# When the expert weights are laid out, and where layer 1's gate is folded, in a two-layer attention and mixture-of-experts kernel

## The chip, the core and the metric

The kernel runs on one core of one Trainium2 chip, as one launch. The metric is device time in microseconds (us), the median of the runs shown. Engines are named as in the profile: PE (TensorE, matrix products), PEld (its weight loads), DVE (VectorE), ACT (ScalarE), POOL (GpSimd), SP (SyncE, which here only starts transfers). ACT and POOL start transfers too (ACTq, POOLq). SBUF is the on-chip memory with 128 partitions; PSUM holds the results of PE in eight banks.

## What is computed

The input `x` holds 8 sequences of 256 tokens with 512 features, in float32. Two layers are added to it, one after the other.

```python
x = x + ffn0(attention(x, Wq, Wk, Wv, Wo, norms, cached keys and values, table, kv_lens))
x = x + moe1(lora(x, W, A, B, scalings, adapter_idx))

# ffn0: each token takes its best 2 of 8 experts, weights rw by softmax
weighted = (softmax(expert_atom_weights) @ atoms) * sigmoid(importance)   # (8, 4096)
vals = einsum('tk,tks->ts', rw, weighted[top_idx])
out = xt @ W.T + segment_sum((xt[:, mask_idx % H] * vals).T, mask_idx // H).T

# moe1: gate by softmax, best 2 of 8 experts
h = gelu(einsum('th,ehi->eti', x, fc1_w) + fc1_b)
y = einsum('eti,eih->eth', h, fc2_w) + fc2_b
out = einsum('eth,te->th', y, combine)
```

So layer 0's expert `e` is a dense 512 x 512 matrix (`W.T` plus 4096 scattered entries of its own), and layer 1's input passes a projection with a low-rank adapter chosen per sequence.

## The kernel before

**Start.** Token tiles hold 128 tokens, so there are 16. `keys_values(i)` (line 908) projects tile `i` to keys and values, four products of 512 columns. `base_weights(i)` spreads the shared matrix `W` over the eight experts into `delta_d`, an array in device memory with experts innermost; `add_delta` (line 882) adds the scattered entries into it by indirect transfers, which run on until batch 5 of attention. Ahead of the first `keys_values`, line 959 transposes the softmaxed `expert_atom_weights` (`pe`) and line 961 copies it to `eawT`, which is first needed by the products at line 978.

**Attention.** A loop over the 8 batches (line 1277) calls `attend(b, 0, ...)` and `attend(b, 1, ...)` (line 1154), each for 128 queries. An `attend` goes through four pairs of heads `m`: scores on PE (line 1162), mask and maximum on DVE (1177), exponential with sum on ACT (1193), division on DVE (1204), transposes on PE (1207) with their copy `pT` on ACT (1211), products with the values on PE (1216) and a copy of the result `oT` on either ACT or DVE (`nc.any`, 1226). Beside it run the queries of batch `b + 2` (up to batch 5), the gate products (`gate_rows`), and the output rows of the first `EARLY = 9` tiles (`output_rows`, line 385: four products into `ph`, an ACT copy to `h`, a transfer to `h_d` from ACT's queue). `start_sums(b - 1)` (line 1268) reads `x` rows and writes them to `sums_d[0]`, where layer 0's output is accumulated.

**Layout of the expert weights.** Layer 0's products need the weights with experts outermost. `load_delta(half, pool, engines)` (line 372) does that for half of the weights in 8 steps: SP reads 512 KB of `delta_d` into a buffer `raw` (line 380), and an engine copies it, transposed within each partition, into `delta[half]` (line 381). The first half is called in batch 6 (line 1285), with ACT's copy alone and three buffers shared with the query inputs; the second half (line 1452) behind the gate's fold, with POOL and ACT in turn and two buffers.

**Between attention and layer 0's slots.** Routing constants; the output rows of tiles 9 and 10; `top2`, `shifted_exp` and `route` (line 136), a long DVE chain that ends in a matrix `put`; inside it the output rows of tiles 11 to 15; then products `pm` (line 250) that give the row numbers `token_i` and the weights of each slot. `fold_gate` (line 1325) follows: layer 1's gate is applied ahead of layer 1's projection, so its weights are folded into it. It loads the projection's weights `wc` (1 MB), transposes them (`pw` to `wn`, lines 1345 and 1346), multiplies them with the gate (`pgw`, 1402), adds the adapters' part (`pga`, 1411) and writes `aTg`; it also prepares the adapters (`aT`, `bT`, `an`, `bn`, `pick`, and `GB` from `pgb`, 1379; `pbg`, 1391).

**Layer 0's slots.** A slot holds 128 routed rows of one expert (line 1489): POOL gathers the rows from `h_d` by `token_i` (`fetched`, line 328), PE transposes them (`pa`, `turned`, 341), eight matmul instructions multiply with `delta` (1501), ACT scales (1511), POOL adds the result into `sums_d` (`added`, 348). Meanwhile SP loads layer 1's weights (`w1`, `w2_0`) and ACT's queue `wc` again. The 36 slots end in a run-time branch (line 1517) for further slots.

**Layer 1.** `sums_d` is read back (line 1544) and added on DVE (1545), transposed (`turn`, 1551), multiplied with `aTg` for the gate's inputs (`inner`, `px`, 1558), then projected (`outer`, 1593). After a second `route`, 36 slots of two products each (lines 1667 and 1695) end the kernel.

**What sets the order.** Each engine has one queue in order. The order is written when the program is built: a planner goes by the place in the program and by when it reckons that inputs are there, and lets later work that it holds for ready pass earlier work. `tc.keep_in_program_order(ins)` ties an instruction behind the one written just before it on the same engine, in issue order only. Memory is reused by tile: a tile waits for the users of the tiles that lay at its addresses.

Of the kernel before, what the change touches and what calls it, by code (L numbers as in the profile page):

```python
# [11 lines left out]
F32 = mybir.dt.float32  # L12
# [41 lines left out]
def two_layer_kernel(ctx: ExitStack, tc: tile.TileContext, io: dict, out: bass.AP):  # L54
# [317 lines left out]
    def load_delta(half, pool, engines, tag="raw", bufs=2):  # L372

        dsrc = delta_d[: D * D, :].rearrange("(c p r) e -> c p r e", p=P, r=D)
        QD = D // 4
        for k in range(HK):
            for j in range(4):
                cols = slice(j * QD, (j + 1) * QD)
                raw = pool.tile([P, QD, E], F32, name="raw", tag=tag, bufs=bufs)
                nc.sync.dma_start(raw, dsrc[half * HK + k][:, cols, :])  # L380
                engines[j % len(engines)](
                    delta[half][:, k, :, cols], raw.rearrange("p r e -> p e r")
                )
# [17 lines left out]
    with ExitStack() as att:  # L401
# [500 lines left out]
        with proj:  # L902
# [55 lines left out]
            pe = psd.tile([P, E], F32, name="pe", tag="psd")  # L958
            nc.tensor.transpose(pe, eaw.rearrange("e h a -> e (h a)"), ident[:E, :E])
            eawT = dp.tile([P, E], F32, name="eawT")  # L960
            nc.scalar.copy(eawT, pe)
            LEAD = 3
            for i in range(LEAD):
                keys_values(i)
                base_weights(i)
            zero_e = dp.tile([P, E], F32, name="zero_e")
# [187 lines left out]
        def attend(b, t, kvs, QT, KT, mask):  # L1154
            oT = oTs[b]
            for m in range(KC):
# [69 lines left out]
                nc.any.tensor_copy(oT[:, m, t * P : (t + 1) * P], po)  # L1226

# [48 lines left out]

        for b in range(B):
# [6 lines left out]
            if b == B - 2:  # L1284
                load_delta(0, xq, (nc.scalar.copy,), tag="xb", bufs=3)
# [3 lines left out]
            if b > 0:  # L1289
                start_sums(b - 1)  # L1290
            if b == B - 1:
                start_sums(b)
            if b == 1:
                for rest in (*sums_d, h_d, g_d):
                    nc.sync.dma_start(rest[N:, :], zero)
            attend(b, 0, kvs, QTs[b], *ready)
# [14 lines left out]
            attend(b, 1, kvs, QTs[b], *now)  # L1311
# [8 lines left out]
    def load_cond(pool):  # L1320
        wc = pool.tile([P, KC, D], F32, name="wc")
        nc.scalar.dma_start(wc, io["w1T"].rearrange("(c p) o -> p c o", p=P))
        return wc

    def fold_gate(fold, ps_t, ps_x):
        wc = load_cond(fold)
# [3 lines left out]
        nc.scalar.dma_start(bT, io["bT"])  # L1330

        wn = fold.tile([P, KC, D], F32, name="wn")
        an = fold.tile([P, D], F32, name="an")
        bn = fold.tile([P, KC, P], F32, name="bn")
        for dst, src in (
            (an, [aT[:, k, :] for k in range(KC)]),
            (bn.rearrange("p c r -> p (c r)"), [bT[:, k * P : (k + 1) * P] for k in range(KC)]),
            *(
                (wn[:, o, :], [wc[:, k, o * P : (o + 1) * P] for k in range(KC)])
                for o in range(KC)  # L1340
            ),
        ):
            pw = ps_t.tile([P, KC, P], F32, name="pw", tag="misc")
            for k in range(KC):
                nc.tensor.transpose(pw[:, k, :], src[k], ident)
            nc.any.tensor_copy(dst, pw.rearrange("p c r -> p (c r)"))
        gw1 = fold.tile([P, KC, E], F32, name="gw1")
        nc.scalar.dma_start(gw1, io["gate1"].rearrange("(c p) e -> p c e", p=P))
# [23 lines left out]
        pick = fold.tile([P, B, BW], F32, name="pick")  # L1372
# [4 lines left out]
        for g in range(B // 4):  # L1377
            pgb = ps_t.tile([P, D], F32, name="pgb", tag="misc")
# [9 lines left out]

        pbg = ps_x.tile([P, E], F32, name="pbg", tag="misc")
# [8 lines left out]
        gwc = fold.tile([P, KC, E], F32, name="gwc")  # L1398
        for d in range(KC):
            pgw = ps_x.tile([P, E], F32, name="pgw", tag="misc")  # L1400
            for k in range(KC):
                nc.tensor.matmul(
                    pgw,
                    wn[:, k, d * P : (d + 1) * P],
                    gw1[:, k, :],
                    start=(k == 0),
                    stop=(k == KC - 1),
                )
            nc.vector.tensor_copy(gwc[:, d, :], pgw)
            pga = ps_x.tile([P, B, BW], F32, name="pga", tag="misc")  # L1410
# [16 lines left out]
    with ExitStack() as ffn:  # L1427
        tp = ffn.enter_context(tc.tile_pool(name="tp0", bufs=1))
        lp = ffn.enter_context(tc.tile_pool(name="lp", bufs=2))
        ps_r = ffn.enter_context(tc.tile_pool(name="ps_r", bufs=1, space=PSUM))  # L1430
        ps_t = ffn.enter_context(tc.tile_pool(name="ps_t", bufs=2, space=PSUM))
        ps_f = ffn.enter_context(tc.tile_pool(name="ps_f", bufs=2, space=PSUM))
# [17 lines left out]
        fold_gate(fp, ps_t, ps_f)  # L1450

        load_delta(1, lp, (nc.gpsimd.tensor_copy, nc.scalar.copy))
# [66 lines left out]
    dst_.close()  # L1519
# [3 lines left out]
    rp = ctx.enter_context(tc.tile_pool(name="rp", bufs=1))  # L1523
# [4 lines left out]
    with ExitStack() as cond:  # L1528
        xtp = cond.enter_context(tc.tile_pool(name="xtp", bufs=1, side="right"))
        x1T = xtp.tile([P, KC, N], F32, name="x1T")  # L1530
        xab = cond.enter_context(tc.tile_pool(name="xab", bufs=4, side="right"))
        ps_t = cond.enter_context(tc.tile_pool(name="ps_t1", bufs=1, space=PSUM))
        ps_l = cond.enter_context(tc.tile_pool(name="ps_l", bufs=1, space=PSUM))
        ps_c = cond.enter_context(tc.tile_pool(name="ps_c", bufs=5, space=PSUM))
# [43 lines left out]
        def outer(q, xa):  # L1578
# [12 lines left out]
            for i, pc in zip(quads[q], pcs):  # L1591
# [8 lines left out]
                g = xab.tile([P, D], F32, name="g", bufs=2)  # L1600
# [213 lines left out]
```

## Time and profile before

| what | value |
|---|---|
| median of 3 runs | 1011.23 us (1009.95 to 1013.35) |
| the profiled execution | 1016.23 us, span of its core 1014.4 us, mean granted PE clock 0.953 |
| busy in the span | PE 942.2, PEld 514.2, DVE 441.1, ACT 382.7, POOL 366.2 us |
| start, keys and values | 0 to 92 us |
| attention, batches 0 to 7 | to 409.7 us |
| up to layer 0's first slot matmul | to 467.98 us |
| layer 0's slots | to 605.9 us |
| up to `outer`'s last product | to 708.5 us |
| layer 1's slots, end | from 724.25 us |
| all transfers | 137.13 MB, mean 135 GB/s |

In a row of the stage table stand the stage (us from the span's start), its length, then for each engine its busy time and, behind an x, its instructions, then the clock granted to PE (1.00 is full), the mean busy share of the 16 DMA engines and what they moved. In a list of waits stand the waiting instruction, its releaser, the total of the waits, how many, and the longest. In a timeline row stand the start, the time from first start to last end, the engine, the line, the operation with its names (out<-in), shapes and count; the bracket gives the idle time of the engine before it and what ended it. Matmuls of float32 appear as several instructions each.

### The profile page before, as it was taken

What the parts mean: (1) busy time and instruction counts of PE and PEld (TensorE: products, weight loads), DVE (VectorE), ACT (ScalarE), POOL (GpSimd) and SP (SyncE); (2) the same over time, 40 slices, a digit from 0 to 9 for tenths busy, and PEclk for the clock granted to TensorE, in tenths of its full rate; (3) what the DMA queues carried; (4) which work ended last, traced back from release to release, by engine and by line L of the source; (5) the groups of instructions that cost most, each with busy time, mean ns of one, the idle gap of its engine ahead of it and who ended that gap; (6) DMA issues with size and microseconds to landing.
All of it is one profiled execution on the core that took longest, in us unless ns stands there. A gap on an engine that the chain in (4) does not pass through costs nothing. (4 is left out here: it accounts for less than half of the span.)

```text
span 1014.4 us, 13280 instructions
## 1 busy us (share of the span) xinstructions
PE 942.2 (93%) x4145; PEld 514.2 (51%) x4145; DVE 441.1 (43%) x1437; ACT 382.7 (38%) x946; POOL 366.2 (36%) x320
## 2 busy tenths in 40 slices
PE   5999889999998899979999985999599999999996
PEld 2655646556555466455444443453245445444542
DVE  5689689855846676832111113440022222222221
ACT  3577356646648878322111111311122222222221
POOL 2622656565463100233667640000233333333321
PEclk9799689999999999998999995999699999999998
DMA  6597492332224600656998759842432333333222
GB/s 186 171 322 276 118 331 60 97 95 74 63 53 120 223 2 1 200 165 206 343 287 158 137 84 296 314 158 73 156 62 55 73 63 61 63 72 63 54 33 38
DMA packets 75654, 137.13 MB, mean 135 GB/s; under 512 B 17710, under 2 KB 23342, under 8 KB 75457
## 3 DMA queue, kind: packets, MB, share of 16 engines
q0 software_dynamic: 25984, 45.26, 23.3%
q1 hardware_dynamic: 38496, 74.57, 21.4%
q10 hardware_dynamic: 11104, 16.44, 4.5%
q8 instruction: 36, 0.59, 0.2%
q14 instruction: 34, 0.27, 0.1%
HBM read 92.05 MB, written 53.61 MB: 144 GB/s over the span
## 5 line engine op out<-in xcount | busy, mean ns | idle before, releaser
L1667 PE MATMUL ph<-w,xsT 128*128 x288 | 131.6, 600 | 0.2 <-issue 0.2
L328 POOL DMA_INDIRECT xs<-g_d,token_i_l x36 | 37.4, 1039 | 258.1 <-PE pa L341 147.0
L1695 PE MATMUL py<-w,hs 128*128 x288 | 129.6, 592 | 0.5 <-ACT hs L1684 0.5
L1501 PE MATMUL py<-delta,xsT 128*128 x288 | 129.1, 593 | 0.3 <-ACT aTg L1414 0.3
L1703 DVE TENSOR_TENSOR y<-py,b 128x512 f32<-128x512 f32 x36 | 24.9, 692 | 211.9 <-PE py L1695 211.9
L343 DVE COPY xsT<-pa 128x512 f32<-128x512 f32 x72 | 49.5, 688 | 150.0 <-PE pa L341 138.7
L1193 ACT ACTIVATE s<-s,mx,roots 128x384 f32<-128x384 f32 x128 | 89.7, 704 | 8.6 <-DVE mx L1189 7.0
L1695 PEld LDWEIGHTS py<-w,hs 128*128 128x128 f32 x288 | 54.6, 190 | 69.2 <-issue 68.2
L1684 ACT ACTIVATE hs<-pu,b 128x128 f32<-128x128 f32 x144 | 41.0, 368 | 116.0 <-PE pu L1681 116.0
L1667 PEld LDWEIGHTS ph<-w,xsT 128*128 128x128 f32 x288 | 52.5, 193 | 52.9 <-issue 52.9
L1501 PEld LDWEIGHTS py<-delta,xsT 128*128 128x128 f32 x288 | 52.1, 190 | 53.6 <-issue 53.1
L913 PE MATMUL pkv<-wkv,xb 128*128 128x512 f32 x128 | 67.1, 650 | 8.8 <-DMA wkv<-wqkvT 8.4
L348 POOL DMA_INDIRECT out<-y,token_i_l x36 | 56.6, 1571 | 48.5 <-DVE y L1706 35.6
L1177 DVE CUSTOM_DVE_ANT_0 s<-ps,mask 128x384 f32<-128x384 f32 x128 | 67.1, 552 | 14.4 <-PE ps L1162 11.9
L348 POOL DMA_INDIRECT sums_d<-y,token_i_l x36 | 56.5, 1570 | 36.9 <-ACT y L1511 22.4
L1216 PE MATMUL po<-pT,kv 128*64 128x128 f32 x768 | 66.1, 285 | 3.4 <-ACT pT L1211 2.3
L1511 ACT ACTIVATE y<-py,weight_l 128x512 f32<-128x512 f32 x36 | 24.7, 687 | 114.1 <-PE py L1501 111.4
L1216 PEld LDWEIGHTS po<-pT,kv 128*64 128x64 f32 x768 | 46.4, 137 | 40.8 <-ACT pT L1211 32.1
L389 PE MATMUL ph<-woT,oT 128*128 128x512 f32 x128 | 60.1, 613 | 5.6 <-ACT h L397 5.6
L1675 ACT COPY h<-ph 128x512 f32<-128x512 f32 x36 | 21.1, 585 | 113.3 <-PE ph L1667 113.3
L1162 PE MATMUL ps<-KT,QT 64*128 64x384 f32 x256 | 58.8, 540 | 4.1 <-DVE mx L1177 4.0
L1211 ACT COPY pT<-pp 128x384 f32<-128x384 f32 x128 | 55.9, 477 | 17.3 <-PE pp L1207 15.5
(353 smaller groups left out, 1497.8 us busy)
## 6 DMA issues: line engine op xcount, KB each, us to landing
delta_d<-spread SPq DMA_DIRECT2D x16, 512.0 KB
raw<-delta_d SPq DMA_DIRECT2D x16, 512.0 KB
w<-fc_w SPq DMA_DIRECT2D x8, 1024.0 KB
w<-fc_w SPq DMA_DIRECT2D x16, 512.0 KB
part<-sums_d SPq DMA_DIRECT2D x32, 256.0 KB
xb<-xT SPq DMA_DIRECT2D x5, 1024.0 KB
sums_d<-zero SPq DMA_DIRECT2D x18, 256.0 KB
kv_new<-kvt ACTq DMA_DIRECT2D x16, 256.0 KB
```

Source lines behind the costliest of these rows:

```text
L343: nc.vector.tensor_copy(xsT, pa)
L348: nc.gpsimd.indirect_dma_start(out=sum_d, out_offset=bass.IndirectOffsetOnAxis(ap=token_i[:, s : s + 1], axis=0), in_=y, in_offset=None, b ...
L389: nc.tensor.matmul(ph, oTs[i // 2][:, k, (i % 2) * P : (i % 2 + 1) * P], woT[:, k, :], start=(k == 0), stop=(k == KC - 1),)
L913: nc.tensor.matmul(pkv, xb[:, k, cols], wkv[:, k, :], start=(k == 0), stop=(k == KC - 1),)
L1162: lambda r=r: nc.tensor.matmul(pss[r], QT[r * HD : (r + 1) * HD, m, t * P : (t + 1) * P], KT[r * HD : (r + 1) * HD, u, t * P : t * P + WU] ...
L1177: nc.vector.tensor_tensor_reduce(out=s, in0=pss[r], in1=mask[:, t, :], scale=1.0, scalar=NEG, op0=ALU.add, op1=ALU.max, accum_out=mx[:, r ...
L1193: nc.scalar.activation(ss[r], ss[r], AF.Exp, bias=mx[:, r : r + 1], scale=root[:, r : r + 1], accum_out=sm[:, r : r + 1],)
L1211: nc.scalar.copy(pT, pp)
L1216: lambda c=c, r=r: nc.tensor.matmul(po[r * HD : (r + 1) * HD, :], kvs[t + c][:, v0 + r * HD : v0 + (r + 1) * HD], pTs[r][:, c * P : (c + 1 ...
L1501: nc.tensor.matmul(py, xsT[:, k, :], delta[k // HK][:, k % HK, bass.ds(own[s], 1), :].rearrange("p a d -> p (a d)"), start=(k == 0), stop= ...
L1667: nc.tensor.matmul(ph, xsT[:, k, :], w1[:, k, bass.ds(own_pe[s], 1), :].rearrange("p a d -> p (a d)"), start=(k == 0), stop=(k == KC - 1),)
L1695: nc.tensor.matmul(py, hs[:, k, :], w2[k // HK][:, k % HK, bass.ds(own_pe[s], 1), :].rearrange("p a d -> p (a d)"), start=(k == 0), stop=( ...
```

## The change

1. `load_delta` becomes a generator. It first starts as many reads as it has buffers, then stops before every copy (`yield`) and starts the next read behind it. With `paced`, the copy is kept in program order.
2. The first half is started in batch 6 and advanced from `attend`, once behind every second pair of heads, in batches 6 and 7 (8 times, for 8 copies). `start_sums` runs one batch earlier, and in batch 5 for batches 5, 6 and 7 at once.
3. The second half gets 8 buffers instead of 2. All its reads are started ahead of the routing constants; its copies stay the last work of the stage.
4. `output_rows` of this stage gets 4 PSUM banks (`ps_f`) instead of 2.
5. `fold_gate` is split. `fold_adapters` stays where it was and does the adapters' part (`an`, `bn`, `pick`, `GB`, `pbg`). The rest (transposes of `wc`, `pgw`, `pga`, `aTg`) runs behind layer 0's slots and takes the `wc` that is loaded during the slots for the projection; the first load of `wc` is gone. It uses eight PSUM banks and two `wn` buffers; the memory of layer 0's weights is given back only behind it.
6. At the start, `pe` and `eawT` come behind the first `keys_values` and `base_weights`.

```diff
-    def load_delta(half, pool, engines, tag="raw", bufs=2):
+    def load_delta(half, pool, engines, bufs, tag="raw", paced=False):
-        for k in range(HK):
-            for j in range(4):
-                cols = slice(j * QD, (j + 1) * QD)
-                raw = pool.tile([P, QD, E], F32, name="raw", tag=tag, bufs=bufs)
-                nc.sync.dma_start(raw, dsrc[half * HK + k][:, cols, :])
-                engines[j % len(engines)](
-                    delta[half][:, k, :, cols], raw.rearrange("p r e -> p e r")
-                )
+        places = [(k, slice(j * QD, (j + 1) * QD)) for k in range(HK) for j in range(4)]
+        raws = []
+        def read():
+            k, cols = places[len(raws)]
+            raw = pool.tile([P, QD, E], F32, name="raw", tag=tag, bufs=bufs)
+            nc.sync.dma_start(raw, dsrc[half * HK + k][:, cols, :])
+            raws.append(raw)
+        for _ in range(bufs):
+            read()
+        for n, (k, cols) in enumerate(places):
+            yield
+            copy = engines[n % len(engines)](
+                delta[half][:, k, :, cols], raws[n].rearrange("p r e -> p e r")
+            )
+            if paced:
+                tc.keep_in_program_order(copy)
+            if len(raws) < len(places):
+                read()
...
-            pe = psd.tile([P, E], F32, name="pe", tag="psd")
-            nc.tensor.transpose(pe, eaw.rearrange("e h a -> e (h a)"), ident[:E, :E])
-            eawT = dp.tile([P, E], F32, name="eawT")
-            nc.scalar.copy(eawT, pe)
             for i in range(LEAD):
                 keys_values(i)
                 base_weights(i)
+                if i == 0:
+                    pe = psd.tile([P, E], F32, name="pe", tag="psd")
+                    nc.tensor.transpose(pe, eaw.rearrange("e h a -> e (h a)"), ident[:E, :E])
+                    eawT = dp.tile([P, E], F32, name="eawT")
+                    nc.scalar.copy(eawT, pe)
...
                 nc.any.tensor_copy(oT[:, m, t * P : (t + 1) * P], po)
+                if m % 2:
+                    next(beside, None)
...
             if b == B - 2:
-                load_delta(0, xq, (nc.scalar.copy,), tag="xb", bufs=3)
+                beside = load_delta(0, xq, (nc.scalar.copy,), 3, tag="xb", paced=True)
+                next(beside)
...
-            if b > 0:
-                start_sums(b - 1)
-            if b == B - 1:
+            if b < B - 2:
                 start_sums(b)
+            if b == B - 3:
+                start_sums(b + 1)
+                start_sums(b + 2)
...
+    def fold_gate(an, gw1, pick, wc, wns, gwc, psum, banks):
+        pgw = [psum.tile([P, E], F32, name="pgw", tag="acc", bufs=KC) for d in range(KC)]
+        for o in range(KC):
+            wn = wns.tile([P, D], F32, name="wn", tag="g", bufs=2)
+            other_side([wc[:, k, o * P : (o + 1) * P] for k in range(KC)], wn, *banks[o])
+            for d in range(KC):
+                nc.tensor.matmul(
+                    pgw[d],
+                    wn[:, d * P : (d + 1) * P],
+                    gw1[:, o, :],
+                    start=(o == 0),
+                    stop=(o == KC - 1),
+                )
         for d in range(KC):
...
-            nc.vector.tensor_copy(gwc[:, d, :], pgw)
-            pga = ps_x.tile([P, B, BW], F32, name="pga", tag="misc")
+            nc.vector.tensor_copy(gwc[:, d, :], pgw[d])
+            bank, tag = banks[d]
+            pga = bank.tile([P, B, BW], F32, name="pga", tag=tag)
...
-        lp = ffn.enter_context(tc.tile_pool(name="lp", bufs=2))
+        lp = ffn.enter_context(tc.tile_pool(name="lp", bufs=1))
-        ps_f = ffn.enter_context(tc.tile_pool(name="ps_f", bufs=2, space=PSUM))
+        ps_f = ffn.enter_context(tc.tile_pool(name="ps_f", bufs=4, space=PSUM))
+        relayout = load_delta(1, lp, (nc.gpsimd.tensor_copy, nc.scalar.copy), 8)
+        next(relayout)
...
-        fold_gate(fp, ps_t, ps_f)
-
-        load_delta(1, lp, (nc.gpsimd.tensor_copy, nc.scalar.copy))
+        folding = fold_adapters(rp0, fp, ps_t)
+
+        for _ in relayout:
+            pass
...
-    dst_.close()
...
+        with tc.tile_pool(name="ps_g", bufs=1, space=PSUM) as ps_g:
+            gwc = xab.tile([P, KC, E], F32, name="gwc", bufs=1)
+            banks = [(ps_t, "pt"), (ps_g, "misc"), (ps_l, "route_a"), (ps_l, "route_b")]
+            fold_gate(*folding, wc, xab, gwc, ps_g, banks)
+        dst_.close()
```

`other_side` holds the four transposes and the copy (`nc.any`) that `fold_gate` had in line.

## Prediction

> **What bounds the kernel now.** I read the stage table first, then the idle time, then each engine's queue in the stages that the diff touches. TensorE (PE) is busy for 942 of 1014 us, so only PE's holes and slow-clock stretches can be won. Columns: stage, its length, busy us of each engine, granted clock, DMA share, GB/s.
>
> ```profile
> core 0: us, PE busy (x) PEld busy (x) DVE busy (x) ACT busy (x) POOL busy (x), PEclk, DMA share, GB/s
> 323.60:337.60 14.00, 11.22 (x34) 5.31 (x33) 6.13 (x18) 12.27 (x16) 3.04 (x4) 0.88 0.65 209
> 337.60:350.00 12.40, 10.18 (x82) 6.40 (x83) 6.54 (x20) 11.27 (x19) 3.25 (x2) 1.00 0.68 213
> 350.00:365.00 15.00, 13.78 (x116) 9.23 (x113) 12.86 (x52) 11.50 (x31) 0.00 (x0) 1.00 0.27 101
> 365.00:388.80 23.80, 23.80 (x206) 16.40 (x205) 16.19 (x66) 19.04 (x53) 0.00 (x0) 1.00 0.00 1
> 388.80:409.70 20.90, 20.01 (x178) 13.49 (x177) 11.99 (x49) 16.11 (x46) 0.52 (x3) 1.00 0.01 2
> ...
> 430.00:440.00 10.00, 5.95 (x11) 2.61 (x12) 2.29 (x2) 2.74 (x3) 4.30 (x2) 0.89 0.64 177
> 450.00:460.00 10.00, 7.87 (x42) 5.89 (x42) 2.91 (x12) 2.34 (x4) 4.10 (x4) 0.74 0.44 125
> ...
> 608.00:612.00 4.00, 0.00 (x0) 0.00 (x0) 0.00 (x0) 0.00 (x0) 0.47 (x1) 0.56 0.65 102
> 616.00:620.00 4.00, 2.23 (x8) 1.43 (x8) 1.72 (x3) 1.17 (x2) 0.00 (x0) 0.50 1.02 313
> ```
>
> The first five rows are batches 5 (three rows), 6 and 7 of attention: PE is idle for 6.2 us in batch 5 and for 0.9 us in the other two. Then come the stage before layer 0's slots and the gap behind them, with PE idle and its clock at half. Who waits for whom from 300 to 470 us:
>
> ```profile
> ACT delta L381 <- DMA raw<-delta_d: 21.4, 8, 5.0
> DVE hot L243 <- PE pm L250: 13.1, 6, 11.7
> PEld ph L389 <- ACT h L397: 8.1, 3, 4.6
> POOL xs L328 <- DVE wn L1346: 6.8, 1, 6.8
> ```
>
> They form one chain: two raw buffers hold the reads back, so ACT stands at a layout copy that waits for its read; the copies of `h` stand behind it; PE waits for them in `ph`; routing's `pm` is queued on PE behind `ph`; the row numbers come out of `pm`. The timelines of PE and DVE show the rest:
>
> ```profile
> 14.38 0.24 PE L959 MATMUL pe<-ident,eaw 8*128 8x8 f32 x1 [2.22 <-DVE place L1006]
> 442.98 1.91 PE L250 MATMUL pm<-put,hot 128*128 128x78 f32 x16
> 455.66 0.44 PE L341 MATMUL pa<-ident,xs 128*128 128x128 f32 x1 [1.89 <-issue]
> 467.98 2.38 PE L1501 MATMUL py<-delta,xsT 128*128 x5 [0.26 <-ACT aTg L1414]
> 616.39 1.11 PE L1551 MATMUL pt<-ident,part 128*128 128x128 f32 x4 [10.52 <-DVE part L1545]
> ```
>
> ```profile
> 418.19 2.01 DVE L300 TENSOR_TENSOR coef<-coef,sm_l 128x128 f32<-128x128 f32 x1
> 424.40 2.02 DVE L189 TENSOR_SCALAR rows_i<-rows_i 128x32 int32<-128x32 int32 x1
> ```
>
> The first rows have arrived at 455.66, yet the first slot matmul starts at 467.98, behind the last `aTg` of the gate's fold.
>
> **1. The softmax transpose at the start.** `pe` stands on PE between the fourth and fifth matmul of the first token tile and idles PE for 2.2 us. Behind `keys_values(0)` its input is long there. The clock also recovers sooner: after the hole PE ran at half clock from 14.55 to 18.04. Gain at least 2.2, at most 2.2 + 1.7 = 3.9; I take 3. PE has no other hole before 92 us, so it passes on.
>
> **2. First half of the weights, paced by heads.** The eight ACT copies (2.05 us each, 16.4) now fall in batch 5, beside query matmuls, and cost its 6.2 us of PE idle and some slow clock: gain 6.5. They move to batches 6 and 7, one behind every second head, the eighth behind the last head of all. There PE is full and ACT has 19.04 + 16.11 = 35.15 of 44.7 us. Seven copies make 49.5; the 13 ACT copies of `oT` there (0.25 each), which may go to either engine, make it 46.2 if DVE takes them. So ACT becomes the bound: +1.5 to +4.8 if it never idles, +14.4 if every copy shows in full. I take +5, near the low end, because batch 5's copies cost PE only 0.8 us each, and the pin of a copy reaches back to one earlier ACT instruction, so a ready exponential may pass it. Net -1.5, between -5 and +8. The `x` rows' start moves one batch earlier, with three batches at once in batch 5: on SP it stands ahead of the raw reads, but those reads are first needed a batch later. The later raw reads each wait on SP for a copy; nothing urgent is queued behind them. Both at nothing; were the cover gone, the 11 us that SP spent on `x` reads and writes (340 to 351) would be the price.
>
> **3. Second half from 8 buffers, four `ph` banks.** All eight 512 KB reads go out at about 410. The stage 468 to 480 moved 304 GB/s; at that rate 4.2 MB plus 0.5 MB of adapters need 15.5 us, so the last lands near 426 instead of 441.7. The seven `ph` rows are 56 matmuls at 0.43 us (8 took 3.60 at L389): 24.1 us plus 1.5 of routing's small ones, from 409.7 to 435.3, where they ended at 443.
>
> Against that: both DVE rows of 2 us lie under a POOL layout copy (418.02 to 420.05, 424.21 to 426.38); L189's twin in layer 1, with no copy beside it, took 0.17. [...] all four POOL copies now fall inside routing's DVE chain. By the rows, two more hits of 1.8 us put its end at 432.3 + 3.6 = 435.9[...]. Then `pm` takes the 7.8 us it took (442.98 to 450.8), and the row numbers are ready at 444 instead of 451.
>
> **4. The gate's fold leaves this stage.** Removed here: `pw` of the weights 2.9, `pgw` 4.5, `pga` 2.7 us of PE, with their copies and the 1 MB load of `wc`. From row numbers to first slot matmul took 16.9 us. What must stay: 1.0 to the gather, 3.6 until the first rows turn on PE (452.06 to 455.66), 0.6 for four transposes, 1.2 for the copy and its hand-overs: 6.4. `pgb` (3.6) and `pbg` (1.0) fit in the gather's wait. First slot matmul: 450.4, 17.6 earlier. I give back 1.6 for a cold clock and for fc1's loads, which start sooner and meet the first gathers: 16, between 11 and 19. The slots (3.85 us each, PE full) only shift.
>
> **5. The fold behind the slots.** PE has a hole of 10.5 us there while the last sums land and are read; the fold is 10.1 us of PE by its rows at a partly cold clock, some 8 warm. It starts when the last slot's banks are free, about 607, and its transposes, copies and products alternate: end 615 to 619, against `turn` at 616.4 and `inner`, the first reader of `aTg`, at 623.6. The clock: it read 0.50 from 612 to 628. [...] Then the first quad ends 1.7 and `px` 0.85 us sooner, no more since the parts still come at the DMA's pace. By the trace alone, with the clock lost anyway, the fold adds 0 to 4. I take -2, between -4 and +4.
>
> **Sum.** -3 - 1.5 - 16 - 2 = -22.5 on the profiled execution (1016.2 us, span 1014.4), giving a span of 992. That execution is 5 us above the median of the runs; the same saving on the median 1011.2 gives 989.
>
> **Rivals.**
> - *ACT-bound tail of attention* (15%): all seven copies show, +14.4 - 6.5 = +8 in part 2. Total -13: 998. For it: ACT's 35 of 44.7. Against: PE lost only 0.8 us per copy before.
> - *The fold delays layer 1* (10%): rows read into the weights' memory wait for the fold or the clock stays cold; part 5 costs +6 instead of -2. Total -14.5: 997. Against: `wc` was loaded at 443.83 while older buffers were still in use, so waits go by tile.
> - *POOL holds DVE longer* (10%): four hits and late reads put the row numbers at 448. Total -18.5: 993.
> - *Pinned copies drain the heads' pipeline* (5%, slower): if no later head's exponentials pass a pinned copy, PE stands for copy 2.05, two exponentials 1.8 and DVE's 0.9, less 0.9 of scores: 3.85 a copy, 31 for eight. Total -3 + 31 - 6.5 - 16 - 2 = +3.5: 1015. It turns slower above 3.5 us a copy. Against it is the one-instruction pin.
> - *It doesn't do what it says* (5%): the reads cannot start before attention's last buffers are free and share bandwidth with `h`, so part 3 gains little; removing the fold still gives 10: about 996.
>
> **Numbers.** The forecast has 55%. Its own range is 983 to 995; 8 in 10 reaches up through the first three rivals: 981 to 1002. A measurement here tells 0.3% (3 us) from no change: faster 0.92, same 0.03, slower 0.05.
>
> **What would show it.** Right: no PE hole at 12 us; first `py` of the slots 16 to 20 us earlier net of attention's shift; no ACT wait for raw above 2 us; `pw`, `pgw`, `pga` in the hole behind the slots, with the clock near 1.0 at `turn`. Wrong: PE idle above 10 us in batches 6 and 7, DVE rows of 2 us four times or more, or `inner` waiting for `aTg`.

## Result and profile after

| | median, us | ratio to before, 95% interval |
|---|---|---|
| before, beside it | 1012.28 (4 runs) | |
| after | 1000.88 (4 runs) | 0.9886 [0.9859, 0.9912] |
| after, measured once more | 1004.47 (9 runs) | 0.9925 [0.9893, 0.9958] |

The change is worth 8 to 11 us, a third to a half of the 22 that were forecast. The direction held. The size did not: the first figure, 1001, lies outside the forecast's own range (983 to 995) and just inside the wide one (981 to 1002), and the second, 0.9925 of 1011.2 or 1004, lies outside both. The profiled execution took 1001.5 us (span 999.8, clock 0.959). Its milestones, in us from the span's start (all but the last are starts), beside those of before:

| what | before | after | stage before | stage after | forecast for the stage |
|---|---|---|---|---|---|
| last key/value product | 90.3 | 87.0 | 90.3 | 87.0 | -3 |
| first gate product of attention | 163.4 | 158.2 | 73.1 | 71.2 | 0 |
| last gate product of attention | 410.7 | 406.9 | 247.3 | 248.7 | -1.5 |
| row numbers ready | 450.8 | 444.9 | 40.1 | 38.0 | -7 |
| first slot matmul | 468.0 | 455.8 | 17.2 | 10.9 | -9 (10.6 less 1.6) |
| last slot matmul | 605.3 | 595.0 | 137.3 | 139.2 | 0 |
| first `turn` | 616.4 | 606.0 | 11.1 | 11.0 | 0 |
| last `outer` product | 707.9 | 696.3 | 91.5 | 90.3 | -2 |
| layer 1's first slot matmul | 724.2 | 709.9 | 16.3 | 13.6 | 0 |
| end | 1014.4 | 999.8 | 290.2 | 289.9 | 0 |

Against the forecast, 1 to 5 us each are missing in attention, in the stage behind it, from the row numbers to the first slot matmul, in the slots and behind them; one stage, the way into layer 1, gained 2.7 that nobody forecast. The timeline of PE in the kernel after, with the answers to the rows shown of before (start, length, operation; the bracket is idle time and what ended it):

```profile
14.91 0.22 PE L977 MATMUL pe<-ident,eaw 8*128 8x8 f32 x1
...
407.53 10.10 PE L402 MATMUL ph<-woT,oT 128*128 128x512 f32 x16 [0.26 <-DVE lg L1254]
420.82 16.47 PE L402 MATMUL ph<-woT,oT 128*128 128x512 f32 x38
437.13 1.91 PE L250 MATMUL pm<-put,hot 128*128 128x78 f32 x16
...
451.88 1.09 PE L341 MATMUL pa<-ident,xs 128*128 128x128 f32 x4 [5.06 <-issue]
452.76 1.71 PE L1407 MATMUL pbg<-gw,bn 128*128 128x8 f32 x8
454.33 1.09 PE L341 MATMUL pa<-ident,xs 128*128 128x128 f32 x4
455.82 4.71 PE L1527 MATMUL py<-delta,xsT 128*128 x8 [0.40 <-DVE low_i L108]
606.03 1.06 PE L1581 MATMUL pt<-ident,part 128*128 128x128 f32 x4
```

The hole in front of `pe` is gone, and so is the one in front of `pt`. The products of 512 columns around `pe` began 0.85 to 1.01 us apart, where PE did not wait, up to 17.27 us in the kernel before and 0.43 us apart from 18.04; in the kernel after they are 0.43 us apart from 15.60 (the trace's clock records begin only at 17.9 and 14.2 us). New is that work of the same size takes longer: 16 instructions of `ph` take 10.10 us where 38 take 16.47 (0.63 against 0.43 each), and the first slot takes 4.71 us where a later one takes 3.60. The stage table of the same execution says why (stage, length, busy us of each engine, granted clock, DMA share, GB/s):

```profile
402.00:406.00 4.00, 2.99 (x26) 2.40 (x26) 1.08 (x4) 2.67 (x3) 0.31 (x1) 1.00 0.08 8
406.00:410.00 4.00, 3.74 (x12) 2.35 (x12) 3.46 (x25) 0.13 (x1) 1.58 (x9) 0.59 0.65 170
410.00:414.00 4.00, 4.00 (x6) 1.54 (x5) 3.10 (x12) 0.00 (x0) 2.05 (x1) 0.56 1.02 379
414.00:418.00 4.00, 4.00 (x13) 2.00 (x12) 0.90 (x3) 3.08 (x4) 2.20 (x2) 1.00 1.03 406
...
446.00:450.00 4.00, 0.82 (x2) 0.00 (x0) 0.00 (x0) 1.09 (x2) 3.23 (x7) 1.00 0.86 267
450.00:454.00 4.00, 2.12 (x11) 2.15 (x11) 0.69 (x1) 0.00 (x0) 2.03 (x3) 0.64 0.78 257
454.00:458.00 4.00, 3.60 (x10) 2.17 (x10) 3.38 (x20) 0.00 (x0) 1.60 (x3) 0.51 0.48 94
```

In both places PE is granted about half its clock (0.56 to 0.59, and 0.51 to 0.64). In the kernel before, the clock was low earlier, during the fold, and full when the slots began at 467.98:

```profile
454.00:458.00 4.00, 2.34 (x9) 1.99 (x10) 0.74 (x6) 0.58 (x1) 2.47 (x3) 0.61 0.70 193
458.00:462.00 4.00, 4.00 (x10) 2.29 (x9) 0.17 (x1) 1.17 (x2) 0.00 (x0) 0.54 0.20 61
462.00:466.00 4.00, 4.00 (x34) 3.75 (x33) 1.99 (x6) 1.03 (x3) 1.59 (x2) 1.00 0.18 42
```

The waits that the forecast named are gone: in the list of waits from 300 to 470 us of the kernel after, ACT's wait for `raw`, 21.4 us before, does not occur, and POOL's is down to 7.3 us in all.

### The profile page after: what moved, and what is told of

The parts are those of the page before. It is cut to its first block, busy times and chain, and to the rows that moved or that the text cites. A ratio compares the mean times of both kernels' runs of the same rounds, so it can differ in the third digit from the quotient of the medians.

```text
span 999.8 us, 13283 instructions
## 1 busy us (share of the span) xinstructions
PE 940.0 (94%) x4145; PEld 514.0 (51%) x4145; DVE 439.9 (44%) x1439; ACT 382.1 (38%) x944; POOL 367.1 (37%) x320
## 5 line engine op out<-in xcount | busy, mean ns | idle before, releaser
L1221 PE MATMUL pp<-ident,s 128*128 128x128 f32 x384 | 59.7, 283 | 2.5 <-DVE s L1218 2.5
```

What stands on the lines that cost most here:

```text
L1221: nc.tensor.transpose(pp[:, c * P : (c + 1) * P], s[:, c * P : (c + 1) * P], ident)
```

## Experiments

The runs of one kernel spread by up to 15 us, mostly with the mean granted clock: the executions of `e2_two_bufs` go from 997.1 us at 0.967 to 1011.15 us at 0.953. So each experiment is read twice, by its ratio to before and by its stages. Those of the profiled executions, one for each run (us; first to last gate product is "attention"):

| run | ratio [95%] | attention | last gate product to row numbers | row numbers to first slot matmul | slots | last `outer` to layer 1 |
|---|---|---|---|---|---|---|
| before | 1 | 247.3 | 40.1 | 17.2 | 137.3 | 16.3 |
| after, first | 0.9886 | 248.7 | 38.0 | 10.9 | 139.2 | 13.6 |
| e13_after_again | 0.9925 | 248.1 | 36.8 | 10.9 | 140.1 | 13.3 |
| e1_unpaced | 0.9847 [0.9811, 0.9883] | 247.5 | 34.9 | 11.0 | 139.3 | 13.4 |
| e2_two_bufs | 0.9889 [0.9841, 0.9938] | 249.0 | 34.3 | 11.4 | 140.4 | 13.5 |
| e9_two_banks | 0.9916 [0.9895, 0.9937] | 253.3 | 38.2 | 11.0 | 140.1 | 13.5 |
| e10_no_part3 | 0.9953 [0.9931, 0.9976] | 250.1 | 42.0 | 10.9 | 139.9 | 13.5 |
| e3_fold_back | 1.001 [0.9984, 1.0035] | 251.6 | 35.4 | 21.2 | 137.3 | 13.8 |
| e15_all_but_fold | 0.9956 [0.9934, 0.9978] | 245.7 | 33.2 | 26.4 | 139.6 | 13.4 |
| e4_start_only | 0.9968 [0.9954, 0.9982] | 249.4 | 38.6 | 18.0 | 137.3 | 16.5 |
| e6_swap_pools | 0.9966 [0.9948, 0.9984] | 246.4 | 40.9 | 15.7 | 137.3 | 13.8 |
| e5_b2_behind | 0.9894 [0.9855, 0.9933] | 250.2 | 37.8 | 10.9 | 140.7 | 10.3 |
| e7_dense_wait | 0.9947 [0.9925, 0.9969] | 248.3 | 38.4 | 17.1 | 138.1 | 13.2 |
| e12_dense_early | 0.9943 [0.9923, 0.9962] | 248.4 | 36.8 | 17.2 | 137.7 | 13.6 |
| e8_dense_hole | 1.0052 [1.003, 1.0075] | 251.0 | 36.4 | 26.2 | 140.1 | 13.4 |
| e11_best | 0.9791 [0.9759, 0.9824] | 247.6 | 34.9 | 9.1 | 140.5 | 10.3 |
| e14_best_dense | 0.9768 [0.9726, 0.981] | 245.7 | 33.2 | 8.4 | 138.2 | 10.3 |

### Undoing one part, or doing one alone

The pacing, undone in the kernel after:

```diff
-                beside = load_delta(0, xq, (nc.scalar.copy,), 3, tag="xb", paced=True)
-                next(beside)
+                for _ in load_delta(0, xq, (nc.scalar.copy,), 3, tag="xb"):
+                    pass
```

(`start_sums` is as before, too.)

> The changed kernel with the first half of the weights laid out as before (one burst, start of the x rows as before); everything else stays changed. Measured so far: batches 5 to 7 gained nothing from the pacing (they ended 1.2 us later net of the start), and the seven ph rows behind them began at a clock of 0.50 (16 matmuls in 10.1 us instead of 6.9). Theory A, clock: the paced copies make ACT the bound, PE runs with holes, its clock drops and the rows start cold; without pacing, attention ends within 1.5 us of the changed kernel, the first 16 matmuls of ph take 7 us, the row numbers come 3 to 4 us sooner after attention's end, and the whole is 2 to 4 us faster than the changed kernel (about 997 to 999). [...] The forecast itself (pacing worth 1.5 us) expects 1.5 us slower.

The ratio, 0.9847, is some 4 us below the first figure of the kernel after (the intervals overlap) and 8 below the second, so the pacing costs where the forecast had a small gain. Batches 6 and 7 in the stage table of the kernel after:

```profile
365.00:385.00 20.00, 17.80 (x154) 12.13 (x148) 13.52 (x55) 19.10 (x43) 0.00 (x0) 1.00 0.26 80
385.00:400.00 15.00, 12.22 (x104) 7.80 (x102) 8.56 (x35) 15.00 (x30) 0.00 (x0) 1.00 0.12 37
```

and with the pacing undone (`e1_unpaced`):

```profile
365.00:385.00 20.00, 20.00 (x177) 13.66 (x173) 15.03 (x61) 16.49 (x48) 0.00 (x0) 1.00 0.00 1
385.00:400.00 15.00, 14.41 (x130) 9.20 (x126) 10.99 (x45) 13.81 (x40) 0.31 (x1) 1.00 0.01 2
```

The fourth number is ACT's share: with the paced copies it is busy for 15.00 of 15.00 us, and PE (first number) for 12.22. ACT has become the bound. The run puts `start_sums` back as well, so it doesn't tell the earlier start of the x rows from the pacing; ACT's full row speaks for the copies. From gate product to gate product, averaged over the profiled executions, the batches took:

| us | batch 5 | batch 6 | batch 7 |
|---|---|---|---|
| seven without the pacing | 41.1 | 23.8 | 21.0 |
| ten with it | 35.8 | 26.9 | 26.1 |

Batch 5 won 5.3 us, and batches 6 and 7 lost 8.3 together; the earlier batches agree within 0.3. Over all profiled executions here, attention takes 249.9 us on average in the ten paced ones and 247.1 in the seven others, and with part 3 in place the next stage takes 37.1 us in the seven paced and 34.1 in the four others: 2.8 and 3.0 us.

Part 3 (`8` back to `2` in the second `load_delta`; `bufs=4` back to `bufs=2` in `ps_f`), one number at a time and both:

> The changed kernel with 2 buffers instead of 8 for the second half of the weights. If the buffers broke the chain from raw reads over ACT to ph and pm, as forecast, two buffers bring it back: ACT waits of 3 to 5 us for raw, pm from 3 to 7 us later, total 1004 to 1008. Theory A, clock: the rows run cold at first and four PSUM banks hide part of ACT's waits, so the buffers are worth less, 0 to 3 us: total 1001 to 1004. [...]

> The kernel after, with two banks for ph again and the eight buffers kept. Together with the run with two buffers and four banks (1.0 of the kernel after in time, 34.3 us from attention's last gate product to the row numbers) it tells buffers from banks. Theory: the banks carry what part 3 has (PE may run two tiles further ahead of the copies of h), the early reads are worth little, so this stage goes back to 37 to 40 us and the total to about 0.991 to 0.994 of the kernel before. Rival: either is enough, since with early reads ACT does not stand at a layout copy; then the stage stays at 34 to 36 us at full clock and the total at 0.9886.

> The kernel after, with two buffers and two banks, so without part 3. The forecast had 7 us for this part: the row numbers would be ready 7 us later than in the kernel after and the ratio 0.995 or 0.996. Theory now (part 3 gives about 2 to 4 us and loses some of it to a cold clock at the stage's start): 38 to 40 us from the last gate product to the row numbers and a ratio of 0.990 to 0.993.

With neither, the time rises to 0.9953, 3 to 7 us above the kernel after, and the forecast's chain is back in the timeline of PE (`e10_no_part3`):

```profile
416.58 9.86 PE L402 MATMUL ph<-woT,oT 128*128 128x512 f32 x22
429.21 5.27 PE L402 MATMUL ph<-woT,oT 128*128 128x512 f32 x8 [2.77 <-ACT h L410]
437.40 3.70 PE L402 MATMUL ph<-woT,oT 128*128 128x512 f32 x8 [2.92 <-ACT h L410]
```

With the four banks alone (`e2_two_bufs`) the same products run in one piece:

```profile
407.30 7.13 PE L402 MATMUL ph<-woT,oT 128*128 128x512 f32 x16 [0.26 <-DVE lg L1254]
414.60 1.02 PE L402 MATMUL ph<-woT,oT 128*128 128x512 f32 x2
416.97 16.47 PE L402 MATMUL ph<-woT,oT 128*128 128x512 f32 x38
```

although ACT still waits 14.2 us for `raw` there, and the ratio, 0.9889, is that of the kernel after. So the banks are enough: ACT may stand at a layout copy as long as PE has somewhere to write. The eight buffers without the banks (`e9_two_banks`) end the waits for `h` as well:

```profile
424.10 17.89 PE L402 MATMUL ph<-woT,oT 128*128 128x512 f32 x38
```

Its stage still takes 38.2 us. But it runs at a clock of 0.50 to 0.84 from 404 to 416 us and of 0.81 to 0.85 from 420 to 430, where `e2_two_bufs` has 1.00, and PE waits 3.2 us for routing's small products. So either half of part 3 breaks the chain; what the eight buffers are worth at a full clock is not shown. Both together give no more than the banks.

The fold, put back whole ahead of the slots (`fold_gate` with a `wc` of its own, called behind `fold_adapters`), with the pacing and without:

> The changed kernel with the whole fold of the gate put back ahead of layer 0's slots (wc loaded there too), all else changed. The forecast's part 4 put the fold at 10.6 us between row numbers and first slot matmul (16.9 against 6.4), and its part 5 put the fold behind the slots at -2. If so: first slot matmul 10 us later, the gap behind the slots as before, total 1010 to 1013. Theory A, clock: only part of it is the fold, since what remains runs cold and waits for the gather (10.9 us were measured, not 6.4); 6 us later and nothing at the other place: total 1005 to 1008.

> The kernel after with the whole fold put back ahead of layer 0's slots and the pacing undone, so that against the kernel before it has the softmax transpose, the pool order and part 3 (eight buffers, four banks). Theory (part 3 is hidden while the fold stands behind the row numbers): the row numbers come 4 to 6 us earlier and the first slot matmul doesn't follow; only the transpose (3.2 us) and the pool order (3.4 us) remain, a ratio of 0.993 to 0.995. Rival (part 3 adds its own): 0.987 to 0.989.

`e3_fold_back` starts its first slot 9.8 us later than the kernel after, and its ratio of 1.001 is the one forecast. That doesn't prove the forecast's 10.6 us for the fold: the row numbers come 4.7 us sooner than before there, and the way from them to the first slot takes 4 us more than before. In `e15_all_but_fold` the row numbers come after 33.2 us, 6.9 sooner than before, as part 3 was meant to, and the first slot matmul comes 26.4 us after them instead of 17.2. Its timeline of PE there, and then the stage table:

```profile
444.01 1.09 PE L341 MATMUL pa<-ident,xs 128*128 128x128 f32 x4 [5.23 <-issue]
...
455.45 1.71 PE L1422 MATMUL pgw<-gw,wn 128*128 128x8 f32 x8
...
459.79 2.91 PE L1433 MATMUL pga<-pick,an 128*128 128x256 f32 x6
463.33 11.94 PE L1529 MATMUL py<-delta,xsT 128*128 x22 [0.63 <-ACT aTg L1436]
```

```profile
440.00:444.00 4.00, 0.00 (x0) 0.02 (x1) 0.00 (x0) 0.00 (x0) 2.93 (x3) 1.00 0.98 345
444.00:448.00 4.00, 3.99 (x20) 4.00 (x21) 1.85 (x9) 0.00 (x0) 0.99 (x1) 0.50 0.50 159
448.00:452.00 4.00, 4.00 (x21) 3.99 (x21) 0.69 (x1) 0.83 (x2) 1.99 (x2) 0.50 0.36 94
452.00:456.00 4.00, 4.00 (x22) 4.00 (x20) 0.69 (x1) 0.80 (x2) 0.00 (x0) 0.50 0.13 47
456.00:460.00 4.00, 4.00 (x18) 3.71 (x19) 0.66 (x5) 0.50 (x2) 1.00 (x1) 0.50 0.00 0
```

With the fold behind the row numbers, part 3 is worth nothing: PE first waits 5.23 us for the gather, at a clock that reads 1.00 up to 444 us, and then does the fold at 0.50 (eight `pgw` in 1.71 us; in `e3_fold_back` at full clock 0.96). The ratio is what the transpose and the pool order (below) give. So part 3 pays only with part 4, and a sum of single undoings counts some of it twice. Part 4 pays without part 3: in `e10_no_part3` the way to the first slot and the slots together take 150.8 us, and 154.2 on average in the three executions with neither part (`before`, `e4_start_only`, `e6_swap_pools`).

The softmax transpose alone:

> The kernel before with only the softmax transpose moved behind the first keys and values. Forecast: 3 us faster (2.2 to 3.9). The trace of the changed kernel shows 3.3 us at 90 us and 5.2 us at batch 0's gate products; if the extra 1.9 us belong to it too, 5 us faster: 1007; if they came from elsewhere, 1009.

0.9968 is 3.2 us of 1015: the forecast's 3.

The change also opens the pool `xab` ahead of `xtp`, which the forecast passed over. That exchange alone, in the kernel before:

> The kernel before, with only the order of two memory pools ahead of layer 1 exchanged (xab, the buffers of g, ahead of xtp, the transposed rows), as the change did in passing. Theory: this alone starts the fc2_b load earlier and brings the 2.7 us between the last projection product and layer 1's first slot matmul (16.3 to 13.6), so a ratio of about 0.997 to the kernel before. Rival: the 2.7 us come from the fold's move or from the memory that is given back later, and this run stays at 1.000 with 16.3 us there.

It gives 0.9966 and 13.8 instead of 16.3 us ahead of layer 1 as expected, but not by an earlier load: it starts 3.6 us behind the last projection product there, and 0.7 before. The traces put it down to a 2 MB load (`fc2_b`, here `b<-fc_b`). What memory it waits for is not known; its place against the last write of `g_d` is what differs. In the kernel before (one view, SP, ACT, POOL and PE in turn) it starts ahead of the last write of `g_d`, and the gather that needs that write starts 8.9 us behind it:

```profile
708.60 0.34 SPq L1650 DMA_DIRECT2D b<-fc_b  x1
709.12 0.33 ACTq L1602 DMA_DIRECT2D g_d<-g  x1
718.04 1.07 POOL L328 DMA_INDIRECT xs<-g_d,token_i_l  x1 [109.57 <-issue]
721.65 1.09 PE L341 MATMUL pa<-ident,xs 128*128 128x128 f32 x4 [13.18 <-DMA xs<-g_d,token_i_l]
```

In the kernel after (as in `e6_swap_pools`: write 703.49, load 705.81, gather 706.66) the write goes first, the gather follows it by 3.1 us, and then it is the gather that shares the DMA with the load, 7.3 us to its rows:

```profile
697.54 0.33 ACTq L1632 DMA_DIRECT2D g_d<-g  x1
699.80 0.34 SPq L1680 DMA_DIRECT2D b<-fc_b  x1
700.62 1.08 POOL L328 DMA_INDIRECT xs<-g_d,token_i_l  x1 [102.40 <-issue]
707.94 1.94 PE L341 MATMUL pa<-ident,xs 128*128 128x128 f32 x8 [11.05 <-DMA xs<-g_d,token_i_l]
```

Moving the load to POOL's queue, pinned behind the first three gathers:

```diff
-        nc.sync.dma_start(b2..., io["fc2_b"]...)
...
+            if first == 0:
+                tc.keep_in_program_order(nc.gpsimd.dma_start(b2..., io["fc2_b"]...))
```

> The kernel after, with the 2 MB load of fc2_b moved from SP's queue to POOL's, pinned behind the first three gathers of layer 1's slots. Theory: in the kernel after this load is in the way of the first gathers (7.3 us from issue to rows, against 3.6 for one alone), so the time from the last projection product to layer 1's first slot matmul falls from 13.6 to about 10 us and the total by about 3 us, to about 0.985 of the kernel before. Rival: the load is needed soon after anyway (the first addition of fc2_b), so what the gathers win the first additions lose, and the total stays at 0.9886.

The stage shrinks to 10.3 us as expected, and the total of that run doesn't show it (0.9894; its attention took 250.2 us and its slots 140.7). Its interval is too wide to tell; `e11_best` below has the same move in combination.

### What the clock does

Six extra products of 512 columns (results unused), to keep PE busy while it waits for layer 0's first rows, behind `pbg` in one run and behind `pgb` in the other:

> The kernel after with six extra products of 512 columns (5.2 us of PE, results unused) behind pbg, in the time in which PE waits for the first gathered rows of layer 0. Theory of the clock [...]: the first eight slot matmuls run at full clock, 3.5 instead of 4.7 us, and layer 0's slots start up to 2 us earlier, net -1 to -2 us. Rival: the granted clock falls at this place for another reason (what PE did before, not what it does in the wait); then the extra products run at half clock, push the slots back by 1 to 3 us, and the total rises.

> As the run with dense products in the wait for layer 0's first rows, but with the six extra products (5.2 us) ahead of pbg, directly behind pgb, so that they fall in the time in which PE is idle for 5 us. Theory: the clock stays at 1.00 up to the first slot matmul: the first eight take 3.5 instead of 4.7 us, the turns and pbg ahead of them half the time, and row numbers to first slot matmul falls from 10.9 to 9 us or less; total 0.986 to 0.988. Rival: the granted clock falls all the same at 452 to 456; then nothing is gained, and up to 1 us is lost.

Both missed: the planner queued the first turned rows ahead of the extra products, so those ran after the wait, at a clock that from 452 to 456 us was 0.60 in `e7_dense_wait` and 0.50 in `e12_dense_early`, and pushed the slots back by 6 us. They show one thing: in `e12_dense_early` they began at 452.69 at a clock of 0.50, which was 0.91 from 456 to 460 us and 1.00 behind, and the slots that followed took 137.7 us, nearly as in the kernel before.

Ten such products in the hole behind layer 0's slots, with the fold back in its old place:

> The kernel with the whole fold ahead of layer 0's slots (the fold put back), with ten extra products of 512 columns (8.6 us at full clock, results unused) in the hole behind layer 0's last slot. It asks what keeps the clock there: in the kernel after the hole was filled with narrow products and copies, and the clock was at 0.50 from 602 to 618. Theory A [...]: the extra products run at 0.86 us each, the clock is near 1.0 when the first rows are turned, and the time from the first turn to the last projection product falls from 93.4 to 88 to 91 us. Theory B (the clock is lost there for a reason that has nothing to do with how PE is filled): the extra products themselves slow down to twice their time and the turn starts cold, with nothing gained or up to 3 us lost against the kernel with the fold put back.

```profile
616.00:620.00 4.00, 4.00 (x10) 1.71 (x9) 0.00 (x0) 0.00 (x0) 0.14 (x1) 1.00 0.55 68
620.00:624.00 4.00, 3.23 (x8) 1.14 (x6) 0.00 (x0) 0.00 (x0) 0.00 (x0) 1.00 0.00 0
624.00:628.00 4.00, 0.34 (x3) 0.34 (x4) 0.69 (x1) 0.00 (x0) 0.00 (x0) 1.00 0.89 261
628.00:632.00 4.00, 1.52 (x8) 0.91 (x7) 1.40 (x3) 1.17 (x2) 0.00 (x0) 0.58 1.05 396
```

This is that run's stage table. Behind the dense products, which end at 623.23 at a clock of 1.00, PE stands for 4.43 us, and then the clock falls to 0.58, while the turns come, whose rows arrive at the DMA's pace (a share of 1.05, 396 GB/s). The extra work also held back the reads of the sums (they started at 623.35, right behind the last extra product, against 607.18 in `e3_fold_back`; why was not shown). So the hole was not filled to its end, and neither theory is settled. From the first turn to the last projection product it took 91.0 us, inside theory A's 88 to 91, but the executions with nothing put there take 89.1 to 93.4. As built, the extra products cost some 4 us (1.0052 against 1.001).

The fold's own products, of 8 to 256 columns, did not run at the same clock in every run. In `e15_all_but_fold` (table above) it stays at 0.50 for 16 us of rows shown as busy, and in `e8_dense_hole` the same products, from 456.74 to 472.31 us, take as long as there (eight `pgw` in 1.71 or 1.72 us each time). In `e3_fold_back` the same products, in the same order behind a gap of 5.24 us, run at 1.00 from 458 us:

```profile
450.00:454.00 4.00, 2.48 (x13) 2.51 (x13) 0.69 (x1) 0.00 (x0) 2.00 (x2) 0.51 0.68 242
454.00:458.00 4.00, 4.00 (x25) 3.99 (x26) 1.85 (x9) 0.59 (x1) 1.51 (x2) 0.63 0.27 75
458.00:462.00 4.00, 3.98 (x35) 3.64 (x33) 0.69 (x1) 1.29 (x3) 0.49 (x1) 1.00 0.40 122
```

What tells these runs apart is not known.

### A version that beats both

> The kernel after with three edits: the first half of the layout not paced (as before), the fc2_b load behind layer 1's first gathers, and the load of wc behind layer 0's first gathers. Sums of what was measured: pacing cost 3.9 us, the fc2_b load 3.3 us at its place, the wc load at most 1.7 us (5.3 us from gather to first turn, against 3.6 in the kernel before). If they add up: about 0.977 to 0.979 of the kernel before, 990 us. If the loads that are moved only meet the next gathers instead: about 0.984, as without them.

It adds up: 0.9791, 993.66 us. `wc` is loaded on POOL's queue behind layer 0's first gathers, and from gather to first turn it took 3.8 us instead of 5.3. One loss is left: a clock of 0.50 from 448 to 452 us. With four dense products ahead of the first rows, put there by hand this time:

```diff
+        for n in range(2):
+            pf = psum.tile([P, D], F32, name="pf", tag="misc")
+            for k in range(2):
+                with tc.high_priority():
+                    tc.keep_in_program_order(
+                        nc.tensor.matmul(
+                            pf, bT[:, k * P : (k + 1) * P], bT, start=(k == 0), stop=(k == 1)
+                        )
+                    )
```

> The fastest version so far (0.9791) with four extra products of 512 columns (3.5 us of PE, results unused) queued behind pbg and ahead of the first turned rows, so that PE has dense work in the wait for layer 0's first rows; the two earlier tries had these products fall behind the first rows. Theory: in that version the first slot matmuls ran at a clock of 0.50 to 0.67 from 444 to 452 us; with the extra products the clock stays near 1.00, the slots take 137 to 138 instead of 140.5 us, and the total falls by 1 to 3 us, to 0.976 to 0.978. Rival: the clock falls anyway, or the products only push the rows back: no change, or up to 2 us slower.

The timeline of PE in this run:

```profile
438.09 3.70 PE L1414 MATMUL pf<-bT 128*128 128x512 f32 x8
441.63 1.18 PE L341 MATMUL pa<-ident,xs 128*128 128x128 f32 x8
443.91 3.69 PE L1539 MATMUL py<-delta,xsT 128*128 x8 [1.11 <-DVE xsT L343]
```

The first slot takes 3.69 us, the clock is 1.00 in every stretch from 436 to 464 us, row numbers to first slot takes 8.4 and the slots 138.2: 3.0 us less than in `e11_best` by the stages. The ratio, 0.9768, 989.08 us, points the same way but its interval overlaps that of `e11_best`.

The kernel after, unchanged, once more:

> The kernel after, unchanged, measured again. If its first figure holds, 0.9886 within 0.3%, the parts depend on each other. If it comes out at 0.983 or less, the parts simply add up and the first executions were slow ones. In the trace: is the clock low again at the start of the stage behind attention (0.5 to 0.6 at 407 to 414 us)?

0.9925: not 0.983 or less, so the parts do depend on each other, and the first figure was if anything too good. The clock was low again behind attention, if less so (0.79 from 408 to 412 us).

## Why the prediction was right in direction and wrong in size

The forecast had 22.5 us, and the stages give 9.2. Three steps failed: in part 2 the "+5, near the low end" for the paced copies, in part 4 the sum of "6.4" with slots that "only shift", and in part 5 the -2, which stood on the author's estimate that the clock would hold in a filled hole.

- **Part 1** was right: -3.2 us alone.
- **Part 2 failed, in sign.** "I take +5, near the low end, because batch 5's copies cost PE only 0.8 us each", less 6.5 in batch 5: -1.5. Batch 5 won 5.3, but batches 6 and 7 paid 8.3, and over all of attention the pacing costs 2.8 us. The price per copy was read in a batch where ACT had idle time (busy for 35.2 of 41.4 us); here it had little (48.9 of 52.3 in the two batches of the kernel after). The stage behind takes 3.0 us more, for which the forecast had no term. This is the rival of the ACT-bound tail in kind; of the 14.4 us that it put into batches 6 and 7, 8.3 came. The stage behind starts later on ACT and mostly at a low clock. Why the clock falls just there is not settled. It was low in eight of the ten executions with the pacing (0.50 to 0.79 in one stretch of 4 us at least) and full in `e2_two_bufs` and `e10_no_part3`, with two buffers; but it was low in three of the seven without the pacing, too, among them `e4_start_only` (0.60 from 404 to 408 us), whose attention is written as before.
- **Part 3's mechanism was right, its size nearly**: 5.8 us (39.9 on average in the three executions without pacing and without it, 34.1 with), where 7 were forecast. It was put down to the reads alone; the banks alone do it as well. Two DVE rows under POOL's layout copies were long, 2.00 and 1.63 us (the same lines in layer 1, with no copy beside them, took 0.29 and 0.17), not four. DVE did not set the row numbers: its last `put` ended at 432.5 us, and `pm` came on PE at 437.13; in `e9_two_banks` DVE waited 5.6 us at `hot` for `pm`.
- **Part 4 was mis-sized.** From row numbers to first slot matmul "6.4" was the sum, 8 with what was given back; it took 10.9. From the gather to the first turned rows it was 5.3 us, where the sum had 3.6, and from there to the first slot 3.9, where it had 1.8: `pbg`, which was to fit in the gather's wait, ran behind the first rows, the turn of the second slot's rows stood ahead of the first slot, and all of it ran at about half clock (0.51 to 0.64 from 450 to 458 us). The slots, "PE full, only shift", grew by 2.7 (137.3 to 140.0 on average in the seven executions with the fold behind the slots and neither products put in PE's wait nor the load of `wc` moved). Of these 2.7 us, 0.8 are turns of the next slots' rows, which the kernel before had done during the fold, and 1.9 the first slot at a low clock: 5.0 to 6.4 us until the second one starts, against 3.87 later on. The `wc` load beside the gather is 1.5 of the 10.9 (5.3 down to 3.8 in `e11_best`). "1.6 for a cold clock" was the term; `e11_best` and `e14_best_dense`, one execution of each, differ by 3.0 us in it.
- **Part 5**: the fold is hidden, as forecast (11.0 against 11.1 us of gap). The clock was not kept: 0.50 from 602 to 618 us in the kernel after, with PE's rows without a gap above 0.6 us from 594 to 607. The estimate behind the -2 failed there; what the clock goes by was not shown. PE stood for 5.06 us ahead of the first turned rows of the slots, and the clock behind was 0.64 and then 0.51; but behind the slots it fell without such a gap. The fold's products show as busy for 16 us in `e15_all_but_fold`, at 0.50 throughout, and in `e3_fold_back` the same products ran at 1.00 from 458 us.
- **Unforecast**: -2.8 us from a pool's place, because a changed memory order moved a 2 MB load. This was luck, and it makes the total look better than its terms.

Together by stages: -3.2 + 5.8 - 5.8 - 3.2 (16.9 to 11.0, and 2.7 given back) + 0 - 2.8 = -9.2, between the two measurements, -11.4 and -7.6 (0.75% of 1014.22).

## What to carry to other kernels

Before work is put beside a full PE, look which engine is second: at 35 of 44.7 us ACT had no room for 14 more. When work is taken out of a wait, ask during what work PE got its clock back, since the next product pays for it (here 5.0 to 6.4 us from the first slot to the second, against 3.87 later on); a few dense products in the wait can be cheaper than none (four of them, 3.0 us less by the stages of one execution each). And look at what a moved pool or buffer does to the start of large loads: a 2 MB load ahead of a write or beside a gather on the path cost 2.5 and 3.3 us here.

## What the runs showed of the hardware

- Rows shown as busy and the granted clock did not go together: 0.50 for 16 us of the fold's products (8 to 256 columns) in `e15_all_but_fold`. The same products began at 454.64 us in `e3_fold_back` and ran at 1.00 from 458. Six products of 512 columns began at 452.69 in `e12_dense_early`, at 0.50 up to 456 us, then 0.91 up to 460 and 1.00 behind.
- In `e8_dense_hole` PE stood from 623.23 us for 4.43 us; the stretch from 624 to 628 us reads 1.00, and the next one 0.58.
- One 2 MB load ahead of a 256 KB write cost 2.5 us on the path (16.3 against 13.8, `e6_swap_pools`), and beside the gather 3.3 us (13.6 against 10.3, `e5_b2_behind`).
- The spread between executions of one program, up to 15 us, goes mostly with the mean granted clock (`e2_two_bufs`: 997.1 us at 0.967, 1011.15 at 0.953).
